# Routing counts in two products, LayerNorm in single-tile pieces, urgent first experts, and the last group's second experts in two halves

## The chip, the core and the metric

The kernel runs on one core of one Trainium2 chip. The metric is device time in microseconds (us), the median of several runs. Engines: TensorE (PE, matmuls; PEld is its weight load), VectorE (DVE), ScalarE (ACT), GpSimd (POOL), and SyncE (SP), which issues most of the DMAs.

## The reference

The input x is 8 sequences of 256 tokens with 128 features, all in float32. Four layers follow one another, each on the LayerNorm of x and added to x:

```python
x = x + attn_a(layernorm(x))      # 8 heads of 64, softmax over the query axis
x = x + ffn(layernorm(x))         # the "first experts"
x = x + attn_b(layernorm(x))      # 16 heads of 8, rotary positions, page mask
x = x + ffn(layernorm(x))         # the "second experts", same weights
```

The feed-forward layer sends each token to one of 8 experts:

```python
logits = x_flat @ w_gate + b_gate
route_p, route_idx = max(softmax(logits)), argmax(softmax(logits))
h = relu(einsum('nd,edm->enm', x_flat, W1) + b1)      # m = 512
y = einsum('enm,emd->end', h, W2) + b2
out = y[route_idx, arange(n)] * route_p
```

## The kernel before

The 2048 tokens are worked in 4 groups g of 512 tokens (2 sequences, NT = 4 tiles of 128). Tokens of different groups never meet, so the layers of different groups can overlap. Two main flows run on PE one after the other. `flow_a` (line 609) runs the first attention of all groups, head by head: scores S_a, their maxima on DVE, exponentials on ACT, the division on POOL (vh_a), and the products pav_a. `flow_b` (line 1082) runs the second attention in entries (g, b), b being the sequence of the group, four steps each: S_b for the row maxima, ptop_b, ST_b for the exponentials, and acc_b. Everything else is a *side job*: a Python generator that emits some instructions at a time and yields the time at which it can go on.

The order of the instructions on each engine is fixed when the program is written out. The class `Plan` (line 68) keeps an estimated clock for each engine, with prices for operations and HOP = 0.2 us for a hand-over between engines. After each piece of a flow, `fill` lets side jobs step until a budget of planned PE time is used (BESIDE_A = 2.0 us per head, BESIDE_B = 1.75 us per half step). `step_side` (line 466) takes, of the jobs that are due, the one with the lowest rank: CLOSE (end of an attention), PREPARE (`prepare_a`, `prepare_b`: LayerNorm, projections and layout for the next group), SETUP, and then EXPERTS in order of creation. `finish_sides` runs what is left after the flows.

An expert job (`ffn_pieces`, line 812; jobs f0 to f3 for the first experts, e0 to e3 for the second) has these steps:
- LayerNorm (st, mv, rstd by a power on POOL, h), transposed (pt) to hT, gate product pg, and the chosen expert as a 0/1 matrix eq.
- Counting (`before`): one product with the matrix `earlier` gives each token its place among those of its tile; three products with `ones` add the counts of earlier tiles; four more sum all counts, for the check against the capacity CAP of 128 rows per expert. These are 8 matmuls, 16 PE instructions in the trace.
- Scatter: four indirect DMAs on POOL (tx<-hf) put tokens into a DRAM buffer, 512 rows for each expert; the first 128 rows of each were filled with zeros once at the start. There are two such buffers, used in turn. Two DMAs on SP bring 128 rows of each expert back (rows).
- Once the job before has finished its products: turning (prt, rT), for each expert the hidden product H (4 weights of W1, 128 rows), relu on DVE or ACT (for experts 2, 3, 6 and 7 ACT, but in f0 and f1 all on DVE), and the product py with W2. A relu on DVE is a maximum with -b1 (h_f, h_e), so its missing bias, b1 times W2, is added to b2 beforehand (`second_biases`, pc, b2c; the rest uses b2x).
- Way back: ys is stored to DRAM by SP (ox), four indirect DMAs on POOL gather it by token (yg), and DVE adds it to x.

A job may do its LayerNorm, counts and scatter when the job before the previous one has finished its products (line 813). f(g) is created when the attention of group g is closed; e(g) when the second attention of group g is divided and projected (`divide`, line 1192). The first preparation for `flow_b` (`first_b`) waits for f0. If any count exceeded CAP, a dense version of everything would run at the end under `tc.If`.

```python
        ripe = [side for side in sides if side.due <= now]
        if not ripe or plan.next_free(pm, "m", 3) > now:
            return False
        min(ripe, key=lambda side: side.rank).step()
```

Of the kernel before, what the change touches and what calls it, by code (L numbers as in the profile page):

```python
# [17 lines left out]
P = 128  # L18
# [6 lines left out]
def kernel(  # L25
# [38 lines left out]
    TG = NT * P  # L64
    CAP = P


    class Plan:
# [3 lines left out]
        HOP = 0.2  # L72
# [60 lines left out]
        def matmul(self, out, lhsT, rhs, passes):  # L133
# [4 lines left out]
            if form != self.form:  # L138
                price += 0.15
# [3 lines left out]
        def elementwise(self, engine, op, outs, ins):  # L143
            n = max(ap.free_size() for ap in outs + ins)
            if engine == "dve":
                price = 0.08 + 0.00108 * n
                if op == "reciprocal":
                    price = 0.1 + 0.0067 * n
                elif op in ("bn_stats", "bn_aggr"):
                    price = 0.2  # L150
            elif engine == "act":
                price = (0.2 + 0.00078 * n) + (0.1 if len(outs) > 1 else 0.0)
            else:
                price = 0.2 + 0.002 * n if op != "tensor_tensor" or n > 8 else 1.0
# [120 lines left out]

    b2x = const.tile([P, E, D], F32, tag="b2x", name="b2x")
    load(b2x, b2.partition_broadcast(P))

# [18 lines left out]
    region = const.tile([P, E], F32, tag="region", name="region")  # L297
    closer = const.tile([P, E], F32, tag="closer", name="closer")
# [4 lines left out]

    to_expert = [hbm.tile([E, TG, D], F32, tag=f"tx{b}", name=f"tx{b}") for b in range(2)]
    of_expert = [hbm.tile([E * CAP, D], F32, tag=f"ox{b}", name=f"ox{b}") for b in range(2)]
# [4 lines left out]
    def setup_experts():  # L310
        DVE.tensor_scalar(region, first, -float(TG), float(TG * E), ALU.mult, ALU.add)
        DVE.tensor_scalar(
            closer, first, float(TG - CAP), -float((TG - CAP) * E), ALU.mult, ALU.add
        )
        for b in range(2):
            load(
                to_expert[b][:, 0:CAP, :].rearrange("e c d -> c e d"),
                zeros.unsqueeze(1).to_broadcast([P, E, D]),
            )

# [8 lines left out]
    b2c = const.tile([P, E, D], F32, tag="b2c", name="b2c")  # L329

    def second_biases():
        for k in range(E // 4):
            pc = misc(f"pc_{k}")
            for i in range(4):
                e = 4 * k + i
                for m in range(NM):
                    c = e * NM + m
                    PE.matmul(
                        pc[:, ts(i, D)], lhsT=b1T[:, c : c + 1].to_broadcast([P, P]),
                        rhs=W2_sb[:, e, m, :], start=(m == 0), stop=(m == NM - 1),  # L340
                    )
# [1034 lines left out]
```

## Time and profile before

| | us |
|---|---|
| median of 3 runs | 554.19 (551.46 to 554.21) |
| profiled execution, device time | 557.06 |
| its span, first to last instruction | 555.3 |
| PE busy | 447.0 (80%) |
| PE weight load busy | 349.0 (63%) |
| DVE busy | 290.4 (52%) |
| ACT busy | 215.6 (39%) |
| POOL busy | 171.5 (31%) |
| mean granted PE clock | 0.879 |

The profile is of one execution. A page of it gives the busy share of each engine in 40 slices of 13.9 us, in tenths. A table of stretches gives the busy time of each engine between chosen times. The chain of waits follows the last instruction back to what released it: each line has a start, a length and the engine and tile that held the chain; "issue" is time for which the profile shows no cause. All compute instructions have the same source line (a helper), so they are told apart by the names of their tiles. Names that are used below: S_a, pav_a first attention; S_b, ST_b, ptop_b, acc_b second attention; before, tx, rows, prt, H, py, ox, yg the expert jobs, with _f and _e for first and second.

### The profile page before, as it was taken

How to read it: one execution, taken by the hardware profiler on the slowest of the kernel's cores; microseconds unless marked ns; L12 is line 12 of the kernel's file. 1: busy time of each engine (PE TensorE's matmuls, PEld its weight loads, DVE VectorE, ACT ScalarE, POOL GpSimd, SP SyncE). 2: the span in 40 equal slices, each digit the busy share in tenths (PEclk: the TensorE clock that was granted, in tenths of full speed). 3: DMA queues.
4: the chain of work that ended last, by engine and by line, in shares of the span. 5: the costliest groups of instructions: out<-in, count | busy, mean ns of one | idle time of the engine just before them, and what ended most of it. 6: DMA issues, size and time to landing. Idle time of an engine off the chain costs nothing.

```text
span 555.3 us, 13517 instructions
## 1 busy us (share of the span) xinstructions
PE 447.0 (80%) x5694; PEld 349.0 (63%) x5694; DVE 290.4 (52%) x742; ACT 215.6 (39%) x591; POOL 171.5 (31%) x227
## 2 busy tenths in 40 slices
PE   3998769678996499998999997999969997392740
PEld 2775546455895388775677865768847875392740
DVE  2576674556752458546675655666427464222110
ACT  1454563545701133555355534266413433230210
POOL 4032330632406454136404420234260012306020
PEclk9996988879995599999899997699978999596785
DMA  7920000010011301101010010010030001202111
GB/s 218 318 77 4 2 1 3 21 41 2 2 33 45 96 1 50 30 1 39 21 41 1 20 30 11 11 48 2 21 95 21 21 20 39 58 19 77 38 49 34
DMA packets 32644, 23.04 MB, mean 41 GB/s; under 512 B 2712, under 2 KB 29888, under 8 KB 32576
## 3 DMA queue, kind: packets, MB, share of 16 engines
q1 hardware_dynamic: 30528, 17.90, 11.0%
q0 software_dynamic: 2048, 4.20, 2.7%
q8 instruction: 47, 0.77, 0.6%
q14 instruction: 21, 0.17, 0.1%
HBM read 13.70 MB, written 8.39 MB: 40 GB/s over the span
## 4 chain that ended last, share of the span: by engine, by line
PE 64%; DVE 14%; issue 7%; ACT 5%; DMA 4%; POOL 4%; another core or an unknown queue 1%; POOLq 0%; SPq 0%; ACTq 0%; DVEq 0%
PE ST_b L201 8%; PE acc_b L201 7%; PE pq_a L201 6%; PE H_e L201 6%; PE py_e L201 5%; PE H_f L201 5%; PE py_f L201 5%; PE S_a L201 3%; PE prot_b L201 3%; PE S_b L201 3%; ACT ex_a L201 2%; DVE nmax_a L201 2%; DVE top L201 2%; PE ptop_b L201 2%; PE pav_a L201 2%
## 5 line engine op out<-in xcount | busy, mean ns | idle before, releaser
L201 ACT ACTIVATE bex_b<-ST_b 128x768 f32<-128x768 f32 x64 | 51.7, 810 | 99.3 <-PE S_b L201 89.1
L201 DVE TENSOR_REDUCE top<-S_b 128x2 f32<-128x256 f32 (+1 forms) x128 | 65.2, 553 | 39.8 <-PE S_b L201 32.1
L201 PE MATMUL ST_b<-qT_b,kT_b 32*128 32x128 f32 (+1 forms) x512 | 71.3, 368 | 11.1 <-ACT bex_b L201 7.2
L201 ACT ACTIVATE ex_a<-S_a,nmax_a 128x256 f32<-128x256 f32 x128 | 58.8, 476 | 38.8 <-DVE nmax_a L201 22.0
L201 PEld LDWEIGHTS ST_b<-qT_b,kT_b 32*128 32x128 f32 x512 | 52.8, 196 | 26.0 <-ACT bex_b L201 12.4
L201 PE MATMUL S_b<-kT_b,qT_b 32*128 32x128 f32 (+1 forms) x512 | 61.8, 366 | 3.6 <-DVE top L201 3.5
L201 POOL TENSOR_TENSOR vh_a<-vs_a,rden_a 128x512 f32<-128x512 f32 x32 | 33.3, 1044 | 93.2 <-DVE rden_a L201 72.5
L201 PEld LDWEIGHTS S_b<-kT_b,qT_b 32*128 32x128 f32 x512 | 48.1, 196 | 7.2 <-issue 6.8
L201 DVE TENSOR_REDUCE nmax_a<-S_a 128x4 f32<-128x1024 f32 x32 | 38.8, 1214 | 7.9 <-PE S_a L201 7.1
L201 PE MATMUL S_a<-qT_a,kT_a 64*128 64x256 f32 x256 | 37.5, 411 | 4.3 <-ACT ex_a L201 3.6
L201 PE MATMUL H_e<-rT_e,W_sb 128*128 128x128 f32 x256 | 35.6, 290 | 0.0
L201 PE MATMUL H_f<-rT_f,W_sb 128*128 128x128 f32 x256 | 34.0, 278 | 0.0
L201 PEld LDWEIGHTS H_e<-rT_e,W_sb 128*128 128x128 f32 x256 | 33.1, 205 | 1.3 <-issue 0.9
L201 PE MATMUL py_f<-W_sb,h_f 128*128 128x128 f32 x256 | 33.7, 277 | 0.0
L201 PE MATMUL py_e<-W_sb,h_e 128*128 128x128 f32 x256 | 33.3, 276 | 0.0
L201 PEld LDWEIGHTS H_f<-rT_f,W_sb 128*128 128x128 f32 x256 | 31.0, 192 | 2.5 <-issue 2.0
L201 PE MATMUL acc_b<-bex_b,sum_w 128*32 128x128 f32 (+1 forms) x512 | 30.8, 346 | 1.3 <-issue 1.2
L201 PEld LDWEIGHTS py_f<-W_sb,h_f 128*128 128x128 f32 x256 | 30.9, 192 | 1.1 <-issue 0.7
L201 POOL DMA_INDIRECT yg_e<-ox,posi_e x16 | 15.5, 970 | 50.7 <-DMA ox<-ys_e 46.5
L201 PEld LDWEIGHTS py_e<-W_sb,h_e 128*128 128x128 f32 x256 | 30.7, 192 | 0.6 <-issue 0.6
L201 PE MATMUL acc_b<-bex_b,vz 128*32 128x128 f32 (+1 forms) x512 | 30.1, 354 | 0.9 <-issue 0.8
L201 PEld LDWEIGHTS S_a<-qT_a,kT_a 64*128 64x128 f32 x256 | 22.4, 190 | 11.6 <-ACT ex_a L201 5.9
(193 smaller groups left out, 798.2 us busy)
## 6 DMA issues: line engine op xcount, KB each, us to landing
W_sb<-in_L_ffn_W_dram SPq DMA_DIRECT2D x16, 256.0 KB, 6.2
rows_f<-tx SPq DMA_DIRECT2D x8, 256.0 KB, 3.5
ox<-ys_f SPq DMA_DIRECT2D x8, 256.0 KB, 2.4
rows_e<-tx SPq DMA_DIRECT2D x8, 256.0 KB, 2.9
ox<-ys_e SPq DMA_DIRECT2D x8, 256.0 KB, 2.3
x_in<-in_L_attn_a_x_dram SPq DMA_DIRECT2D x4, 256.0 KB, 3.4
tx<-zeros SPq DMA_DIRECT2D x2, 512.0 KB, 8.0
out_dram<-x_e SPq DMA_DIRECT2D x4, 256.0 KB, 2.3
```

The source lines that it names most:

```text
L201: return tc.keep_in_program_order(getattr(self.engine, op)(*args, **kw))
```

## The change

- Counting takes two products over a matrix of 5 columns of blocks: `earlier` with eqs (eq and a zero block), and `ones` with sums, a running sum over tiles that DVE builds by a copy and three additions. The last block of the result is the total count. POOL zeroes one block of eqs and one of sums.
- LayerNorm yields after each tile's statistics and each tile's normalization.
- A rank URGENT is put ahead of all others. f0 gets it, and so does `first_b`. URGENT and CLOSE jobs may step when the filling budget is used up. f(g) is created when group g begins its first attention and waits for its input (x_of); `first_b` is created when group 3 begins its first attention. For it, `prepare_b` adds the extra rows with one DVE instruction instead of ACT and POOL.
- The last group's second experts become two jobs of 256 tokens (2 tiles), e30 and e31, each with 64 rows per expert; `divide` gives the first its input after the group's first entry. e(g) is created when group g begins its second attention.
- Each job has DRAM buffers of its own, with its own zeros loaded at its first step. Experts are worked in pairs. rT has one buffer instead of two. The relu of experts 0, 1, 4 and 5 is on DVE and that of the others on ACT in all jobs, and bias2 takes the place of b2x and b2c, made from four loads and 16 instead of 32 matmuls. Tiles u1 to u3 of the preparation share the three vh buffers of the first attention.
- HOP and some prices of the planner have new values.

```diff
-        HOP = 0.2
+        HOP = 0.3
...
-                price += 0.15
+                price += 0.2
...
+    ROWS = {4: 128, 2: 64}
...
+    def on_vector(e):
+        return e // 2 % 2 == 0
...
     def second_biases():
-        for k in range(E // 4):
-            pc = misc(f"pc_{k}")
-            for i in range(4):
-                e = 4 * k + i
-                for m in range(NM):
-                    c = e * NM + m
-                    PE.matmul(
-                        pc[:, ts(i, D)], lhsT=b1T[:, c : c + 1].to_broadcast([P, P]),
-                        rhs=W2_sb[:, e, m, :], start=(m == 0), stop=(m == NM - 1),
-                    )
...
-            DVE.tensor_tensor(
-                b2c[:, half, :], b2x[:, half, :], pc.rearrange("p (e d) -> p e d", e=4), ALU.add
+        pairs = b2.rearrange("(k i) d -> k i d", i=2)
+        for parts, place, i in PARTS:
+            load(
+                bias2[parts, :, place, :],
+                pairs[:, i, :].partition_broadcast(parts.stop - parts.start),
             )
-            yield
+        yield hop()
+        pc = misc("pc")
+        chosen = [e for e in range(E) if on_vector(e)]
+        for k, e in enumerate(chosen):
+            for m in range(NM):
+                c = e * NM + m
+                PE.matmul(
+                    pc[:, ts(k, D)], lhsT=b1T[:, c : c + 1].to_broadcast([P, P]),
+                    rhs=W2_sb[:, e, m, :], start=(m == 0), stop=(m == NM - 1),
+                )
+        for parts, place, i in PARTS:
+            mine = bias2[parts, 0 : E // 2 : 2, place, :]
...
+            DVE.tensor_tensor(mine, mine, added, ALU.add)
+        yield
...
     sides = []
...
-        if now >= until or max(plan.at["dve"], plan.at["act"]) > now + LATE:
+        if max(plan.at["dve"], plan.at["act"]) > now + LATE or plan.next_free(pm, "m", 3) > now:
             return False
         ripe = [side for side in sides if side.due <= now]
-        if not ripe or plan.next_free(pm, "m", 3) > now:
+        if not ripe:
             return False
-        min(ripe, key=lambda side: side.rank).step()
+        side = min(ripe, key=lambda side: side.rank)
+        if now >= until and side.rank > CLOSE:
+            return False
+        side.step()
...
         for i in range(NT):
             st = sm.tile([P, 6], F32, tag="st", name=f"st_{name}_{i}")
             DVE.bn_stats(st, xt[:, i, :])
             DVE.bn_aggr(mv[:, i, :], st)
+            yield
...
+        PT = 2 * CAP // P
+        to_expert = hbm.tile([E, TL, D], F32, tag=f"tx_{n}", name=f"tx_{n}")
+        of_expert = hbm.tile([E * CAP, D], F32, tag=f"ox_{n}", name=f"ox_{n}")
+        for c in range(0, CAP, P):
+            some = min(P, CAP - c)
+            load(
+                to_expert[:, c : c + some, :].rearrange("e c d -> c e d"),
+                zeros[0:some].unsqueeze(1).to_broadcast([some, E, D]),
+            )
         while computed[0] < turn - 1:
             yield soon()
-        xt, buf = xs[g], turn % 2
-        n = f"{n}{g}"
+        while any(name not in x_of for name, _ in tokens):
+            yield soon()
...
-        lg, d, eq, sc, ex, rk = (small(s) for s in ("lg", "d", "eq", "sc", "gex", "rk"))
+            return t.unsqueeze(1).to_broadcast([P, NL, E])
+        lg, d, sc, ex, rk = (small(s) for s in ("lg", "d", "sc", "gex", "rk"))
+        eqs, sums = (
+            sm.tile([P, NT + 1, E], F32, tag=f"r{s}", name=f"{s}_{n}", bufs=2)[:, 0 : NL + 1, :]
+            for s in ("eq", "sums")
+        )
+        POOL.memset(eqs[:, NL, :], 0.0)
+        POOL.memset(sums[:, 0, :], 0.0)
+        eq = eqs[:, 0:NL, :]
...
+        yield
+        DVE.tensor_copy(sums[:, 1, :], eq[:, 0, :])
+        for i in range(1, NL):
+            DVE.tensor_tensor(sums[:, i + 1, :], sums[:, i, :], eq[:, i, :], ALU.add)
         yield hop()
-        before = misc(f"before_{n}")
-        PE.matmul(
-            before[:, : NT * E], lhsT=earlier, rhs=eq.rearrange("p n e -> p (n e)"),
-            start=True, stop=False,
-        )
-        for i in range(NT - 1):
+        before = misc(f"before_{n}")[:, 0 : (NL + 1) * E]
+        for lhsT, of, start in ((earlier, eqs, True), (ones, sums, False)):
             PE.matmul(
-                before[:, (i + 1) * E : NT * E],
-                lhsT=ones,
-                rhs=eq[:, i : i + 1, :].to_broadcast([P, NT - 1 - i, E]),
-                start=False,
-                stop=(i == NT - 2),
+                before, lhsT=lhsT, rhs=of.rearrange("p n e -> p (n e)"), start=start,
+                stop=not start,
             )
-        counts = before[:, NT * E : (NT + 1) * E]
-        for i in range(NT):
-            PE.matmul(
-                counts, lhsT=ones, rhs=eq[:, i, :], start=(i == 0), stop=(i == NT - 1)
-            )
+        counts = before[:, NL * E : (NL + 1) * E]
         DVE.tensor_tensor(
-            rk, before[:, : NT * E].rearrange("p (n e) -> p n e", e=E), over_tiles(region),
-            ALU.add,
+            rk, before[:, : NL * E].rearrange("p (n e) -> p n e", e=E),
+            over_tiles(region[NL]), ALU.add,
         )
         DVE.tensor_tensor(rk, rk, eq, ALU.mult)
         DVE.tensor_reduce(ps_, rk, AX.X, ALU.add)
...
-        rows = ln.tile([P, E, D], F32, tag="rows", name=f"rows_{n}", bufs=3)
-        for k in range(2):
-            half = slice(k * E // 2, (k + 1) * E // 2)
...
+        pairs = to_expert.rearrange("(k i) c d -> i c k d", i=2)
+        tiles_of = rows[:, 0 : PT * E // 2, :].rearrange("p (k t) d -> p k t d", t=PT)
...
             load(
-                rows[:, half, :],
-                to_expert[buf][half, 0:CAP, :].rearrange("e c d -> c e d"),
+                tiles_of[p0 : p0 + some, :, t, :],
+                pairs[r0 // CAP, r0 % CAP : r0 % CAP + some, :, :],
             )
...
-        rT = ln.tile([P, E * CAP], F32, tag="rT", name=f"rT_{n}", bufs=2)
-        ys = ln.tile([P, E, D], F32, tag="rows", name=f"ys_{n}", bufs=3)
+        rT = ln.tile([P, TILES * P], F32, tag="rT", name=f"rT_{n}", bufs=1)
...
-            h1 = big.tile([P, NM, CAP], F32, tag="h1r", name=f"h1_{n}_{e}", bufs=4)
-            H = misc(f"H_{n}_{e}")
-            for m in range(NM):
...
+            h1 = big.tile([P, NM, P], F32, tag="h1r", name=f"h1_{n}_{e}", bufs=4)
+            some = min(NM, 512 // CAP)
+            for m0 in range(0, NM, some):
+                H = misc(f"H_{n}_{e}_{m0}")
+                for m in range(some):
+                    PE.matmul(
+                        H[:, ts(m, CAP)], lhsT=W1_sb[:, e, ts(m0 + m, P)],
+                        rhs=rT[:, ts(e, CAP)], start=True, stop=True,
+                    )
+                c = e * NM + m0
...
+                for t in range(t0, t1):
+                    r0 = t * P
+                    if r0 // CAP == (r0 + 64) // CAP:
+                        parts = [(h1s[r0 // CAP][:, :, r0 % CAP : r0 % CAP + P], slice(0, P))]
+                    else:
+                        parts = [
+                            (h1s[r // CAP][:, :, r % CAP : r % CAP + 64], slice(p0, p0 + 64))
+                            for r, p0 in ((r0, 0), (r0 + 64, 64))
+                        ]
+                    for m in range(NM):
+                        for part, to in parts:
+                            e = 2 * k + (r0 + to.start) // CAP
+                            PE.matmul(
+                                py[to, ts(t - t0, D)], lhsT=part[:, m, :],
+                                rhs=W2_sb[:, e, m, :], start=(m == 0), stop=(m == NM - 1),
+                            )
...
+        pending = None
+        for k in range(E // 2):
+            h1s = []
+            for e in (2 * k, 2 * k + 1):
+                h1s.append(hidden(e))
+                yield
+            if turns and turns[0] < (k + 2) * PT:
+                turned(turns.pop(0))
+                yield
+            if pending:
+                yield max(plan.over(h1.name) for h1 in pending[1]) + plan.HOP
+                yield from project(*pending)
+            pending = k, h1s
+        yield max(plan.over(h1.name) for h1 in pending[1]) + plan.HOP
+        yield from project(*pending)
         computed[0] += 1
...
+            yield hop() if i == NL - 1 else None
+        at = 0
+        for (name, tiles), xt in zip(tokens, xts):
+            xn = new_x(f"x_{n}_{at}")[:, 0:tiles, :]
...
-                t.append(mid.tile([P, 2, T], F32, tag=f"u{y + 1}", name=f"rt_{n}_{w}_{y}", bufs=1))
+                t.append(mid.tile([P, 2, T], F32, tag="vh", name=f"rt_{n}_{w}_{y}", bufs=3))
...
-            rt = mid.tile([P, 2, T], F32, tag="u3", name=f"rt_{n}_{w}", bufs=1)
+            rt = mid.tile([P, 2, T], F32, tag="vh", name=f"rt_{n}_{w}", bufs=3)
...
-                ACT.mul(xT[:, r, :, :], rt, section[r])
-                yield hop()
-                POOL.tensor_tensor(
-                    xT[:, r, :, :], xT[:, r, :, :],
-                    extra[:, w, r : r + 1, :].to_broadcast([P, 2, T]), ALU.add,
-                )
+                rows = extra[:, w, r : r + 1, :].to_broadcast([P, 2, T])
+                if at_once:
+                    DVE.scalar_tensor_tensor(
+                        xT[:, r, :, :], rt, section[r], rows, ALU.mult, ALU.add
+                    )
+                else:
+                    ACT.mul(xT[:, r, :, :], rt, section[r])
+                    yield hop()
+                    POOL.tensor_tensor(xT[:, r, :, :], xT[:, r, :, :], rows, ALU.add)
...
-            if b == 1:
-                yT = yTs[g].rearrange("p b t -> p (b t)")
-                py = misc(f"py_b{g}")
-                for i in range(NT):
...
+            whole = g != groups[-1] or len(groups) == 1
+            if whole and b == 0:
+                return
+            tiles = range(NT) if whole else range(2 * b, 2 * b + 2)
+            yT = yTs[g].rearrange("p b t -> p (b t)")
+            py = misc(f"py_b{g}_{b}")
+            for k, i in enumerate(tiles):
+                PE.matmul(
+                    py[:, ts(k, P)], lhsT=yT[:, ts(i, P)], rhs=wo_sb, start=True, stop=True
                 )
...
+            some = slice(tiles[0], tiles[-1] + 1)
+            xn = new_x(f"x_b{g}_{b}")[:, 0 : len(tiles), :]
...
+            x_of["e", g if whole else (g, b)] = xn
...
     def first_experts(g):
-        share = set(range(E)) if g < 2 else {0, 1, 4, 5}
-        ready[g] = Side(ffn(g, "f", share, g < 2), EXPERTS + begun_ffn[0])
...
+        def ended(name, rows):
+            x_of["b", name[1]] = rows
+        Side(ffn(f"f{g}", [(("f", g), NT)], ended, g < 2), URGENT if g == 0 else EXPERTS + g)
...
+    def second_experts(name, *tokens):
+        def ended(name, rows):
...
+        Side(ffn(name, tokens, ended, False), EXPERTS + begun_ffn[0])
+    def begun_a(g):
         if g == 0:
             setup_experts()
             ready["bias"] = Side(second_biases(), SETUP)
...
+        first_experts(g)
         if g == NG - 1:
-            ready["first"] = Side(first_b(), PREPARE)
+            ready["first"] = Side(first_b(), URGENT)
+    def begun_b(g):
+        if g < NG - 1:
+            second_experts(f"e{g}", (("e", g), NT))
+            return
+        for b in range(2):
+            second_experts(f"e{g}{b}", (("e", (g, b)), 2))
...
-        return (yield from prepare_b(0))
+        return (yield from prepare_b(0, True))
```

## The prediction

> **What bounds the kernel now.** I read the busy share first, then the same engines by stretch, then the chain that ended last. The page's slices:
>
> ```profile
> PE   3998769678996499998999997999969997392740
> ...
> PEclk9996988879995599999899997699978999596785
> ```
>
> TensorE (PE) is at 9 or near it nearly everywhere, except for three holes: the first slice, slices 13 and 14 (about 165 to 192 us), and the last six (from 472 us). In the holes the granted clock drops to 0.5 too, so what little runs there runs slower. The stretches put numbers on it (columns: length, then busy time of PE, weight load, DVE, ACT, POOL; the last three are clock, DMA share, GB/s):
>
> ```profile
> 13.00:163.00 150.00, 129.34 (x2177) 94.66 (x2174) 93.56 (x215) 74.74 (x283) 44.03 (x51) 0.91 0.16 48
> 163.00:192.00 29.00, 14.69 (x75) 12.62 (x73) 10.41 (x54) 4.57 (x12) 15.25 (x26) 0.59 0.20 58
> 192.00:212.00 20.00, 20.00 (x142) 17.97 (x145) 11.32 (x21) 7.59 (x20) 11.40 (x10) 0.91 0.13 36
> 212.00:467.00 255.00, 236.01 (x2852) 179.64 (x2848) 150.04 (x374) 111.79 (x232) 76.05 (x89) 0.94 0.10 27
> 467.00:500.00 33.00, 21.86 (x170) 20.89 (x166) 10.61 (x32) 8.68 (x25) 5.69 (x10) 0.79 0.11 32
> 500.00:545.00 45.00, 21.30 (x161) 20.40 (x160) 10.17 (x34) 5.96 (x19) 12.51 (x18) 0.72 0.19 53
> 545.00:555.30 10.30, 0.00 (x0) 0.00 (x0) 0.14 (x1) 0.00 (x0) 0.00 (x0) 0.50 0.12 33
> ```
>
> Both attentions (13 to 163 and 212 to 467) are bound by PE with the side work fed in: 86% and 93% busy. Between them stand 49 us, and behind them 88 us, in which a chain of small steps sets the pace. The chain of waits names them:
>
> ```profile
> 168.24 3.36 PE before_f L201 x16
> ...
> 178.51 5.42 issue
> ...
> 188.91 1.06 POOL rstd_b L201
> ...
> 211.81 0.94 PE S_b L201 x16
> ...
> 467.74 3.77 issue
> 471.52 1.01 POOL tx L201
> ...
> 516.60 1.94 PE prt_e L201 x8
> ...
> 534.20 2.28 DMA ox<-ys_e
> ```
>
> The first product of the second attention (S_b) stands at 211.81, because its input is the output of group 0's first experts, and these were served last: their tokens are back in rows at 114, but their products H_f run from 139.5, and POOL normalizes the result (rstd_b) at 188.9, behind eight scatters of groups 1 and 2. The tail is: dispatch of group 2's second experts until 480.7 (13.0), their products until 498.7 (17.9), dispatch of group 3 until 516.6 (17.9), products until 533.7 (17.1), way back until 545.2 (11.5), end (10.1).
>
> **Part 1: urgent first experts.** f0 becomes a side job of the highest rank, created when group 0 begins, and steps past the allotted filling time; b0's preparation (first_b) gets the same rank when group 3 begins, near 118. x_a of group 0 is there near 46 (pt_a at 44.07). Dispatch of f0 takes about 18 (group 3's, above), products 17 if nothing stands between, way back about 10, so x_f0 comes near 95 to 110, before 118. b0's preparation, with extra rows added by one fused DVE instruction instead of ACT and POOL (0.72 + 1.16 each, eight of them), then lies in group 3's attention. So S_b can follow the first attention directly. What f0 moves past: its four scatters (1.28 each) and rstd (1.04) stand on POOL among the heads' vh_a products of group 1 instead of group 2 (105 to 110 now), where POOL is as idle (44 of 150 us); its loads and stores on SP pass only loads that are done by 40. The price there stays what it was: 0.
> Where does that end? Now near 163. Added on PE: b0's transposes, values and rotations, 4 instructions 0.45 (full clock), 8 in 0.9, 8 in 3.5, together about 5. Removed: half of second_biases, one of two blocks of 32 instructions of 3.77 us, on the chain at 23 and 29; and 1.5 of f0's counts (part 2). Taken: plus 3 for new waits, of which two are not in the trace. The rotations' tiles now share the three vh buffers with the heads (bounds 0 to 8: six tiles, each waiting at most for one pav of 1.1 us and the POOL product of 1.04; behind the waiting DVE instruction stand the heads' maxima). And DVE's bias sums now wait for four loads issued near 21 instead of one at 19.4 (0 to 5: the W loads take 6.2 us to land and the zeros 8.0). S_b at 163 + 5 - 3.8 - 1.5 + 3 = 166, instead of 211.8: **-46**.
> That isn't all gain: in those 49 us PE also did f1 and f2's dispatch. At full clock: turning 1.0, H 7.2 (64 instructions, 0.89 per 8), py 7.2, transposes, gates and counts of f1 and f2 3.8. **+19** must be paid again in the second attention, which is dense: 1 for 1.
>
> **Part 2: counts by two products.** Each of eight dispatches issues 16 PE instructions now, 4 after. On the chain 16 cost 1.95 at full clock and 3.36 to 3.5 at half. So 1.5 to 2.6 each are saved. DVE pays a copy and three sums, 0.22 a step on the chain (0.66 to 0.9), beside PE's other work in the attentions and open in the tail. f0 to f2 are counted already; f3, e0, e1, e2 and e3 give 5 x 1.6 = **-8** (bounds -4 to -12). Two POOL memsets (0.09 each, from mark) come into the wait of the product: see the third rival. LayerNorm by single tiles adds no instruction; it only lets other work between.
>
> **Part 3: zeros and buffers.** The zero loads go from 2 to 9, 8.0 us each to landing (half that for a half group), on SP and the DMA engines, which are at 0 to 3 tenths after 42 us. They are issued at a job's first step, before it waits for its input, and the first scatter comes 10 us or more after LayerNorm starts; I take 0. If SP stood behind a waiting store (its waits on ys_f reach 46.1) a scatter would be late by up to 8. Relu of experts 2, 3, 6, 7 of f0 and f1 moves to ACT (4 x 0.37 instead of 0.69 each, 6 us more on ACT per group); ACT has 75 of 150 us there: 0. One rT buffer instead of two: products of two groups never overlap: 0.
>
> **Part 4: the last group in halves.** Per half as many H and py instructions as for a whole group, with 64 rows. H: weights are the same 128x128, and the weight load's row (8 in 0.97) is as long as the matmul's (8 in 1.06), so the 3.6 a half would cost by columns is likelier 6: between 0 and +7.2 for both, taken +5. py: 64 columns wide, two side by side (0 to +7.2, taken +2). Changes of form: 8 py after attention's acc_b take 1.09 in the chain and 0.89 after H, so 0.20 a change, 16 changes: +3.
> The Trainium skill (TensorEngine Tiling (Array Packing), Key Properties) says the same of the last: changing the mode drains TensorE; and its Instruction Overhead gives each matmul about 60 cycles of overhead, so that 64 columns gain little. That speaks against halves; by it, as an estimate, +7 for H would stand in the place of +5. No row here has 64 columns at 128 rows, so nothing in this trace tests it.
> The tail then, from attention's end, if the backlog is the same as now: e2's dispatch 11 (13 less 2 for counts), products 17.9, first half's dispatch 13.5 (17.9 - 2.3 counts + 0.5 sums - 2 scatters of 1.28), its products 11.5 (17 x half, +3), second half's dispatch 11 (2 gathers of 1.26 fewer ahead of it), products 11.5, way back 8.9, end 10.1: 95 with nothing overlapped, 82 with the first half's dispatch behind e2's products. The first half's input is there one entry of attention (some 30 us) before the end, but its rank is below e2's, and e2 is nearly always ready. Middle: 88, as now: **0**.
>
> **Sum.** 555.3 - 46 + 19 - 8 + 0 = 520.3; stalls I haven't placed (the planner's prices and its HOP are all new, so each engine's order changes; the PE holes of 20.7 and 19.0 us inside the attentions could shrink or grow) I leave at +2: span 522. The profiled execution took 557.06 for a span of 555.3; the median of the runs is 554.19, 1.1 below the span. So **521 us**, -6%. Fallback to the dense path is excluded: counted from the reference's inputs, the fullest expert gets 50 tokens of a half (limit 64) and 92 of a group (limit 128).
>
> **Rivals.**
> *The halves overlap.* If f0's early end also drags e0 to e2 forward, so that e2 is done and the first half dispatched when attention ends, the tail is the second half alone: division and LayerNorm 9, dispatch 11, products 11.5, back 8.9, end 10.1, about 51 to 70 for 88: 485 to 508, taken 502. For it: attention takes in side work for only 88 of 255 us. Against: the 19 us of part 1 come first.
> *Moved, not saved.* f1's work pushes e1 past the attention's end; the tail holds e1's products (18) as well and each dispatch is open: 521 + 18 = 539.
> *POOL comes between.* The product of the counts now needs two POOL memsets. POOL is in order, and a job's gathers stand and wait for the store ("POOL yg_e" waits 46.5 us in two stretches for ox). If a memset falls behind four gathers, PE, in order too, waits 2.3 + 4 x 1.26 = 7.3. At all eight later dispatches that is 58: 579, slower. It decides from the fifth on (5 x 7.3 = 36 against 33 gained). Against it: the memsets are emitted with the gate product, some 2 us before the counts, mostly ahead of the gathers.
> *The change doesn't do what it says:* f0 urgent, but b0 still late (S_b near 200): 545; this and the second rival share a place.
>
> **How the numbers follow.** Forecast (510 to 533) 0.50; halves overlap (below 510) 0.20; moved or not urgent in effect (533 to 551) 0.18; POOL between (above 557) 0.08; in the last 0.04 they cancel. Within 0.5% (551.4 to 557.0), about what a measurement of this kernel can tell from none, 0.04. Faster 0.88, slower 0.08. The range, 8 in 10: down to 498, up to 545, from part 4's and the second rival's bounds.
>
> **What would show it.** S_b's first product near 166 and no hole at slices 13 and 14; `before` at 4 instructions a job and about 0.5 us at full clock; the PE holes left only in the tail; py of the halves near 6 us a half; tail 82 to 95. Wrong if PE waits for POOL at `before`, if S_b starts after 190, or if the tail is outside 65 to 105.

## The result and the profile after

The kernel after takes 581.0 us (median of 4 runs, 576.14 to 582.13), before 553.38 in the same series: ratio 1.0487, 95% interval 1.0418 to 1.0557. It is slower by 4.9%; the prediction was 521. The profiled execution took 576.14 for a span of 574.3.

The slices of the page after:

```profile
PE   3879688999777899789799997889959986995690
...
PEclk9999889899886599879799996799988999698555
```

The hole at slices 13 and 14 is narrower, as meant. What is new stands to its right: 7s and 8s among the 9s of slices 16 to 29 (215 to 416 us), where before has one 8 and one 7, and clocks of 6 to 8 beside them. The same stretches as before (length, then busy time of PE, weight load, DVE, ACT, POOL; clock, DMA share, GB/s):

```profile
167.00:183.40 16.40, 8.32 (x142) 5.36 (x140) 14.30 (x33) 5.00 (x24) 7.25 (x10) 0.68 0.00 1
183.40:485.40 302.00, 267.75 (x2970) 201.14 (x2970) 167.45 (x442) 120.01 (x258) 91.22 (x131) 0.89 0.10 30
485.40:510.00 24.60, 20.58 (x148) 19.99 (x148) 9.73 (x33) 6.33 (x21) 2.46 (x5) 0.79 0.16 50
510.00:537.00 27.00, 14.85 (x144) 12.91 (x142) 8.68 (x41) 5.81 (x22) 9.26 (x15) 0.83 0.21 64
537.00:574.30 37.30, 21.85 (x129) 20.30 (x129) 4.06 (x13) 4.17 (x17) 1.93 (x2) 0.55 0.06 16
```

The second attention starts at 183.4 instead of 211.8 (-28.4), but takes 302.0 instead of 255.3 (+46.7); the tail takes 88.9 instead of 88.2. That is +19.0, the whole difference of the spans. In the second attention PE is busy 31.5 us more, idle 34.3 instead of 19.0, and the clock falls from 0.94 to 0.89.

The list of what PE waits for in this stretch (total, times, longest) has three rows that before does not have there at all:

```profile
PE pt_f L203 <- ACT hf_f L203: 4.4, 2, 3.7
PE pt_b L203 <- ACT h_b L203: 4.0, 2, 3.0
PE pt_e L203 <- ACT hf_e L203: 2.4, 3, 1.3
```

PE waits 10.8 us in front of LayerNorm transposes whose rows are still being made. The timeline shows the longest of them:

```profile
240.85 0.79 PE L203 MATMUL prt_f<-ident,rows_f 128*128 128x128 f32 x4
...
244.65 0.13 DVE L203 SCALAR_TENSOR_TENSOR shift_f<-mv_f,rstd_f 128x4 f32<-128x4 f32 x1
244.82 1.65 ACT L203 ACTIVATE hf_f<-x_a,shift_f,rstd_f 128x128 f32<-128x128 f32 x4 [2.56 <-DVE shift_f L203]
...
245.37 1.63 PE L203 MATMUL pt_f<-ident,hf_f 128*128 128x128 f32 x4 [3.73 <-ACT hf_f L203]
```

The transposes stand in PE's written order when not one row of hf_f exists: the first is begun at 244.82. None of the attention's products that are written behind them starts before them, and PE does nothing for 3.73 us; then the four transposes go at ACT's pace (1.63 for four; 0.66 where the rows are ready, pt_b at 236.38 in the mended kernel below).

Why do they stand there? The code of after says it:

```python
        def step(self):
            plan.end = 0.0
            try:
                self.due = max(next(self.gen) or 0.0, plan.at["pe"])
...
    def hop():

        return plan.end + plan.HOP
...
            yield
        yield hop()
        pt = misc(f"pt_{name}")
```

`hop()` is meant to be the planned end of the last instruction of this step plus HOP. With LayerNorm in pieces, the last piece ends its step with a plain `yield`. The next step zeroes `plan.end`, issues nothing, and yields 0 + 0.3: due at once. The planned wait between the normalisation and the transposes is gone. I call it the lost hop.

### The profile page after: what moved, and what is told of

It is laid out like the page before. It is cut to its first block, busy times and chain, and to the rows that moved or that the text cites. A ratio compares the mean times of both kernels' runs of the same rounds, so it can differ in the third digit from the quotient of the medians.

```text
span 574.3 us, 13668 instructions
## 1 busy us (share of the span) xinstructions
PE 468.1 (82%) x5698; PEld 355.4 (62%) x5698; DVE 302.6 (53%) x805; ACT 221.4 (39%) x633; POOL 164.2 (29%) x240
## 5 line engine op out<-in xcount | busy, mean ns | idle before, releaser
L203 DVE TENSOR_REDUCE top<-S_b 128x2 f32<-128x256 f32 (+1 forms) x128 | 65.1, 553 | 47.7 <-PE S_b L203 37.2
L203 PE MATMUL S_b<-kT_b,qT_b 32*128 32x128 f32 (+1 forms) x512 | 69.1, 402 | 6.1 <-DVE top L203 5.5
L203 PE MATMUL H_e<-rT_e,W_sb 128*128 128x128 f32 (+1 forms) x320 | 48.7, 317 | 2.8 <-ACT rT_e L203 2.8
L203 PEld LDWEIGHTS H_e<-rT_e,W_sb 128*128 128x128 f32 x320 | 46.0, 230 | 5.8 <-ACT rT_e L203 4.0
L203 PE MATMUL S_a<-qT_a,kT_a 64*128 64x256 f32 x256 | 43.4, 460 | 7.6 <-ACT ex_a L203 7.1
L203 POOL DMA_INDIRECT yg_e<-ox_e,posi_e x16 | 15.6, 976 | 76.6 <-DMA ox_e<-ys_e 73.0
L203 PEld LDWEIGHTS S_a<-qT_a,kT_a 64*128 64x128 f32 x256 | 25.6, 214 | 17.1 <-ACT ex_a L203 9.0
L203 PE MATMUL pav_a<-ex_a,vh_a 128*32 128x64 f32 x1024 | 24.7, 244 | 12.3 <-POOL vh_a L203 5.5
L203 PE MATMUL py_e<-W_sb,h_e 128*128 128x128 f32 (+1 forms) x320 | 34.6, 304 | 0.0
L203 ACT ACTIVATE h_e<-H_e,b1T 128x128 f32<-128x128 f32 (+1 forms) x80 | 20.5, 354 | 36.0 <-PE H_e L203 36.0
L203 PEld LDWEIGHTS pav_a<-ex_a,vh_a 128*32 128x32 f32 x1024 | 18.8, 123 | 24.8 <-POOL vh_a L203 12.7
L203 PEld LDWEIGHTS py_e<-W_sb,h_e 128*128 128x128 f32 (+1 forms) x320 | 31.9, 187 | 0.7
```

The source lines that it names most:

```text
L203: return tc.keep_in_program_order(getattr(self.engine, op)(*args, **kw))
```

## The experiments

Before itself took 541 to 557 us on the chips used, so kernels are compared by their ratio to before in the same series (95% interval in brackets), and stretches from the profiled executions. "S_b" is the start of the second attention, "B" its length. The ratio of one and the same kernel moved by a point between two chips (0.9696 and 0.98, the counts alone, below), so differences of about a point between two series can't be told from none.

### First series: one part of after undone

*The old planner numbers* (HOP and prices of before):

```diff
-        HOP = 0.3
+        HOP = 0.2
...
-                price += 0.2
+                price += 0.15
...
```

> The kernel after, with the planner's numbers of before alone put back (HOP 0.2, a change of form 0.15, and its old ScalarE, VectorE and GpSimd prices); all instructions are those of after, only their order differs. Theory 1 (the new prices spread the side work wrongly: of the +46.7 us in the second attention 28 are idle gaps and half clock that the written order makes): 555 to 565 us, the stretch from the first S_b to the last acc_b 275 to 285 instead of 302. Theory 2 (the work itself, its place and the buffers it shares are what costs): 576 to 586, the stretch 297 to 307. Theory 3 (the halves of the last group): 576 to 586 as well.

Measured: 1.0512 (1.0488 to 1.0536). The first theory falls: the prices are not what costs.

*No urgency:*

```diff
-        if now >= until and side.rank > CLOSE:
+        if now >= until:
...
-URGENT if g == 0 else EXPERTS + g)
+EXPERTS + g)
...
-            ready["first"] = Side(first_b(), URGENT)
+            ready["first"] = Side(first_b(), PREPARE)
```

> The kernel after, without the urgent rank: first experts of group 0 take rank EXPERTS + 0, the first preparation of the second attention PREPARE, and no side steps past its budget. Theory 1 (prices): 578 to 590, since the first S_b falls back from 183 towards 200 while the second attention keeps its gaps. Theory 2 (the urgent steps push the heads of the first attention aside and leave work for the second): first S_b at 195 to 212, the second attention 302 shorter by 19 to 35, total 565 to 581. Theory 3 (halves): no change beyond 5 us either way.

Measured: 1.0416 (1.0362 to 1.0469). S_b 207.2 instead of 183.4, B 276.4 instead of 302.0: what the urgent rank wins ahead of S_b (23.8) is paid back behind it (25.6).

*The last group whole:*

```diff
-            whole = g != groups[-1] or len(groups) == 1
+            whole = True
...
-        for b in range(2):
-            second_experts(f"e{g}{b}", (("e", (g, b)), 2))
+        second_experts(f"e{g}", (("e", g), NT))
```

> The kernel after, with the last group's second experts and its close in one piece of four tiles as in before; everything else as after. Theory 1 and 2: the tail from the last acc_b to the end stays at 85 to 100 us (88.9 with halves, 88.2 before), the second attention shortens by at most 8 (the first half's work leaves it: its rows, products of 14 us at most), total 572 to 590. Theory 3 (128 hidden products of 64 columns at 350 ns, bound by their weights and at half clock, and two chains of dispatch in place of one are the loss): tail 88 with 25 us of work less elsewhere, total 552 to 562.

Measured: 1.0285 (1.0256 to 1.0315), tail 87.9 against 88.9. The halves fill 13 us of the tail's idle time (44.5 whole, 31.7 halved) with 14 us more of PE work. Faster than after, as the first two theories allowed; the next series shows whether that lasts.

*Experts one at a time* in whole groups, three pending:

```diff
...
+            for e in range(E):
+                queue.append((e, hidden(e)))
+                yield
+                if len(queue) == 3:
+                    yield from project_next()
...
```

> The kernel after, with the experts of all whole groups taken one at a time with three pending, and both transposes ahead of them, as in before (the second products of a pair of experts came in one step of 16 products in after); the halves stay in pairs. Theory 1 (prices): within 8 us of 581. Theory 2 in its sharper form (a step of 16 products, about 4.5 us in one go, starves the attentions between their heads): 560 to 572, the gaps and the half-clock time of the second attention (34.3 and 64.6) halfway back to 19.2 and 30.7. Theory 3: within 5 us of 581.

Measured: 1.0701 (1.0666 to 1.0736). All three theories missed: slower, B 302.7, tail 107.0 with a clock of 0.60. None of the four brings after back to before.

### Second series: the lost hop

*The hop mended*, everything else as after:

```diff
-            yield
+            if i < NT - 1:
+                yield
         yield hop()
```

> The kernel after, with one line changed: the LayerNorm on ScalarE or VectorE still comes in pieces of one tile, but the last piece does not end its step, so that the hop to the transposes is counted from that piece. Theory L (in after the step behind the last piece issues nothing, its hop is counted from a zeroed end, and the transposes are put into PE's order before their rows are there: 10.8 us of waits of pt_f, pt_b and pt_e in the second attention, none in before): these waits fall below 3 us, the stretch from S_b to the last acc_b from 302 to 285 to 293, total 564 to 573. Rival O (the wait only moves to the next product that PE needs, since the rows come no sooner): the waits fall, the stretch stays within 5 of 302, total 576 to 584.

Measured: 1.0017 (0.9975 to 1.006), 556.6 us: more than expected, 4.7 points by two lines. The stretches of the mended kernel, the one row of transposes left in PE's waits in its second attention, and the largest row there:

```profile
20.70:184.00 163.30, 126.73 (x2135) 91.08 (x2135) 106.09 (x281) 83.33 (x315) 57.63 (x76) 0.92 0.19 54
184.00:463.80 279.80, 256.83 (x2950) 195.61 (x2950) 168.38 (x434) 117.38 (x253) 86.76 (x120) 0.91 0.10 30
463.80:554.70 90.90, 65.83 (x419) 60.44 (x419) 21.49 (x75) 16.25 (x58) 13.55 (x22) 0.63 0.13 37
```

```profile
PE pg_e L203 <- ACT hT_e L203: 7.3, 2, 5.2
...
PE pt_f L203 <- ACT hf_f L203: 1.8, 1, 1.8
```

S_b stays at 184.0; B falls by 22.2. Of these, 11.3 are idle time (34.3 to 23.0) and 8.5 are speed: PE spends 47.7 us at half clock instead of 64.6. The theory that the wait only moves (rival O) is right in a small part: 7.3 us of waits stand now in front of the gate product pg_e, 0 in after. In the longest, 5.2, the copy hT_e stands on ACT behind gex_e, which waits for d_e on POOL, behind four scatters (455.58 to 460.45).

*LayerNorm undivided* (both piece-wise `yield` lines taken out):

```diff
             DVE.bn_aggr(mv[:, i, :], st)
-            yield
...
-            yield
         yield hop()
```

> The kernel after with the LayerNorm undivided: no step ends between its statistics or between its four normalisations, as in before. Theory L: the same gain as with the last hop mended, within 4 us of that kernel (564 to 573). A theory of its own (pieces as such help: shorter steps let the attention's reductions and exponentials in between): slower than the mended kernel by 4 to 12 us. Rival O: 576 to 584.

Measured: 1.0074 (1.0046 to 1.0103), 4 us above the mended kernel. Undoing the pieces also restores the hop; pieces as such are worth little.

*Mended and whole* (both edits above): 

> The kernel after, with the last hop of the LayerNorm mended and the last group's second experts whole. If the two losses are separate (11 us for the halves by the ratios 1.0487 and 1.0285, and 8 to 17 for the lost hop): 553 to 562. If the order alone decides and both were chance: 568 to 578.

Measured: 1.0 (0.9957 to 1.0044), as the mended kernel with halves. The halves' 2 points of the first series do not add: on the mended kernel they are worth nothing either way.

*The pieces alone, on before:*

```diff
             DVE.bn_aggr(mv[:, i, :], st)
+            yield
...
                     bias=shift[:, i : i + 1], scale=rstd[:, i : i + 1],
                 )
+            yield
         yield hop()
```

> The kernel before, with the LayerNorm in pieces as in after and nothing else. Theory L: waits of the transposes behind their rows appear in the second attention (0 us in before), 6 to 12 us of them, total 562 to 572 where before has 554 to 557. Rival O: within 4 us of before.

Measured: 1.0222 (1.018 to 1.0264), with 9.8 us of transposes' waits in B where before has none:

```profile
PE pt_f L201 <- ACT hf_f L201: 4.8, 1, 4.8
...
PE pt_e L201 <- ACT hf_e L201: 2.8, 3, 1.7
...
PE pt_b L201 <- ACT h_b L201: 2.2, 2, 1.9
```

So these waits come with the lost hop from both sides; with the pieces and their hop on before (third series) no such row stands in the second attention. The price of the hop is shown on after alone: in the 12 us here the pieces themselves have a share, since with their hop they cost 9 us on the counts base.

### Third series: counts, zeros and urgency

*Mended, without urgency* (the edits of both kernels above):

> The kernel after with the last hop of the LayerNorm mended (556.6 us) and without the urgent rank. Theory M (urgency moves work and saves none: the 27.8 us that the first S_b comes earlier are paid again in the second attention, 24.5, and in the tail, 2.7): first S_b at 198 to 210, the second attention 255 to 268, total 551 to 561. Rival W (urgent first experts are worth what the first S_b gains, and something else in after eats it): total 570 to 584.

Measured: 1.0099 (1.0054 to 1.0144); S_b 205.2, B 269.4, tail 83.6. Mended with urgency it was 1.0017. Theory M holds within a point, with B 1.4 above its range.

*The counts alone, on before:*

```diff
...
+        POOL.memset(eqs[:, NT, :], 0.0)
+        POOL.memset(sums[:, 0, :], 0.0)
...
+        for lhsT, of, start in ((earlier, eqs, True), (ones, sums, False)):
+            PE.matmul(
+                before, lhsT=lhsT, rhs=of.rearrange("p n e -> p (n e)"), start=start,
+                stop=not start,
+            )
...
```

> The kernel before with the counts by two products over a running sum and nothing else. By the prediction's term (30 of 32 products of 0.2 to 0.6 us leave PE, 22.5 us of records to 8): 543 to 553, against 555 for before. Rival O (PE waits for the longer chain on VectorE and for the zeros that GpSimd writes): 553 to 563.

Measured: 536.5 us, 0.9696 (0.9617 to 0.9774). More than the term: B 242.1 instead of 255.3, half clock in it 13.7 us instead of 30.7.

*Mended, the zeros written by VectorE:*

```diff
-        POOL.memset(eqs[:, NL, :], 0.0)
-        POOL.memset(sums[:, 0, :], 0.0)
+        DVE.memset(eqs[:, NL, :], 0.0)
+        DVE.memset(sums[:, 0, :], 0.0)
```

> The kernel after with the last hop mended, and the two zeroed columns of every dispatch written by VectorE instead of GpSimd. If the zeros behind the gathers on GpSimd hold up the counts (the third rival of the prediction): the waits of before_e and before_f behind eq and sums go, 546 to 553. If they do not matter: within 3 us of 556.6.

Measured: 1.0116 (1.0074 to 1.0158): no gain. The one wait of `before` behind POOL in the mended kernel (3.5 us) is gone, the time is not: the zeros behind the gathers do not decide.

*Counts and mended pieces on before* (the edits shown above, together):

> The kernel before with two parts of the change: the counts by two products, and the LayerNorm in pieces with the hop counted from its last piece. If the two parts add (counts -2 to -12, pieces with their hop -5 to +2): 541 to 555, and faster than both kernels. If any change of the written order costs as much as it brings: 554 to 564.

Measured: 0.9855 (0.9775 to 0.9935). Faster than both kernels, but slower than the counts alone (545.5 against 536.5 us in the same series): the pieces bring nothing even with their hop.

### Fourth series: single parts on the counts base

With the hop mended after is still 2 to 3 points above before with the counts. Each of the next kernels adds one part to that base. Urgency:

```diff
...
-        ready[g] = Side(ffn(g, "f", share, g < 2), EXPERTS + begun_ffn[0])
+        ready[g] = Side(job, URGENT if g == 0 else EXPERTS + begun_ffn[0])
...
```

> The kernel before with the two-product counts (536.5 us), and with the urgent part alone: first experts of group 0 and the first preparation of the second attention in the urgent rank, the rule that urgent steps may pass their budget, and the first preparation's columns made at once on VectorE. Theory M (moved, not saved): first S_b 20 to 30 us earlier than 206.5, the second attention longer by as much, total 532 to 541. Theory P (the prediction's term: 46 won, 19 paid): 505 to 515. Theory U (urgency is the 20 us that after still lacks): 546 to 560.

Measured: 1.0024 (0.9997 to 1.0051). S_b 187.3, B 268.9.

The planner's numbers of after:

```diff
-        HOP = 0.2
+        HOP = 0.3
...
```

> The kernel before with the two-product counts, and the planner's numbers of after (HOP 0.3 and the new prices). If these write the worse order: 545 to 560. If they do not matter: 533 to 541.

Measured: 0.9841 (0.9793 to 0.9889): no loss that can be told.

Experts in pairs:

```diff
...
+        def project_pair(k, h1s):
+            yield max(plan.over(h1.name) for h1 in h1s) + plan.HOP
+            for e, h1 in zip((2 * k, 2 * k + 1), h1s):
+                project(e, h1)
+            yield
...
```

> The kernel before with the two-product counts, and the experts taken in pairs as in after: 16 second products in one step, the second transposes behind the first pair. If the long steps hold up the attentions: 542 to 556, with more waits and more half clock in the second attention (17.1 and 13.7 us). If the pairs help, as the run with single experts in after (595 against 581) says: 526 to 536.

Measured: 1.0109 (1.0063 to 1.0156). B 256.5.

Shared buffers:

```diff
-tag=f"u{y + 1}", name=f"rt_{n}_{w}_{y}", bufs=1
+tag="vh", name=f"rt_{n}_{w}_{y}", bufs=3
...
-tag="rT", name=f"rT_{n}", bufs=2
+tag="rT", name=f"rT_{n}", bufs=1
```

> The kernel before with the two-product counts, and the shared buffers of after: the rotated products of the second attention's preparation in the three buffers of vh, one buffer in place of two for the turned rows of the experts. If the sharing is what after lacks: 545 to 558, with waits of pav behind vh or of rt behind pav in the first attention's last group. If not: 533 to 541.

Measured: 0.9769 (0.9722 to 0.9815), the lowest median of all, 529.2 us, and 7% below after (1.0487) by ratio. Against the counts base (0.9696 and, on another chip, 0.98) sharing costs nothing.

### Fifth series: the pairs taken from the mended kernel

Both edits (hop mended, experts one at a time) on after, and the counts base on the same chip:

> The kernel after with the last hop mended, and the experts of whole groups taken one at a time with three pending. If the pairs' long steps are what the mended kernel still lacks: its ratio to before falls from 1.002 to 0.965 to 0.985. If the worth of pairs hangs on the order around them (they cost 19 us on the counts base and brought 14 on after): ratio 0.99 to 1.03.

> The kernel before with the two-product counts, once more, on the chip that runs the kernel beside it: ratio 0.965 to 0.980 to before; with it the gap of the mended kernel to the counts base is read on one chip.

Measured: 0.9855 (0.977 to 0.994) and 0.98 (0.9746 to 0.9854). The gap is closed to half a point. The stretches of the first, from S_b on:

```profile
178.70:423.80 245.10, 232.81 (x2889) 179.34 (x2889) 158.99 (x409) 114.55 (x241) 76.79 (x102) 0.99 0.09 29
423.80:529.60 105.80, 64.90 (x481) 60.11 (x477) 26.70 (x103) 20.32 (x70) 23.06 (x39) 0.70 0.15 46
```

and of the counts base:

```profile
207.20:444.40 237.20, 222.30 (x2800) 169.75 (x2801) 154.14 (x391) 114.02 (x242) 79.05 (x99) 0.97 0.10 29
444.40:529.00 84.60, 39.51 (x301) 37.43 (x301) 22.39 (x75) 14.66 (x44) 18.29 (x30) 0.73 0.16 45
```

With both mends B holds f1 and f2's work in 245.1 us at a clock of 0.99, 57 us less than after. The early S_b is then real: the attention ends 20.6 us before that of the counts base. The tail takes 21.2 more, because the second experts of the later groups are no further: when the attention ends, the last of e1's products are still running, and all of e2, e30 and e31 stands behind it: e2's hidden products start 22 us after the end, where those of the counts base start 15 after it, and the last half's at 489.9.

## Why the prediction was wrong, step by step

Three steps failed. The one that made the kernel slower is the LayerNorm in pieces, which the prediction had at nothing: "LayerNorm by single tiles adds no instruction; it only lets other work between", and beside it "stalls I haven't placed ... I leave at +2". No instruction was added, but a wait in the written order was taken away. Measured: +25 us in after (1.0487 against 1.0017). Among kernels with single experts the lost hop is worth more, 8 points (1.0701 against 0.9855). It could have been read from the diff: a bare `yield` now stands ahead of `yield hop()`, and what `hop` adds to is zeroed at each step.

With the hop mended the kernel is only as fast as before, so two more steps are needed for the gain that did not come. The largest is the term for urgency, -46 + 19 = -27: what it wins ahead of S_b is paid again in full behind it (-23.8 and +25.6 in after), and by ratio it is worth between -0.8 and +2.2 points. The other was not priced at all: experts in pairs, 16 second products in one step. They cost 3 points on the counts base (1.0109 against 0.98, and against 0.9769 on the same chip) and 1.6 on the mended kernel (1.0017 against 0.9855, on two chips). In the kernel with the lost hop they brought 2 points; why the sign turns there is not settled.

Point by point:
- *S_b at 166* (-46): 183.4 (-28.4). "x_a of group 0 is there near 46 (pt_a at 44.07)" misread a row: that pt_a is the LayerNorm transpose of group 1. The closing of group 0's attention, also named pt_a but fed by yT_a, is at 71, and the first tile of x_f0 is added at 136.5 instead of 95 to 110 (before 183.3). S_b follows the last pav_a directly, as predicted, but the first attention itself ends at 183.4 instead of 158.6. I had added 5 for b0's preparation and 3 for waits. PE shows 8.3 and 10.5 there, 6.0 more of f0's and f1's work, and 7.7 more in S_a and pav_a themselves; 7.7 less in other rows, 3.7 of it in second_biases, stand against these.
- *+19 paid again:* the first experts' work on PE in B rose from 37.5 to 55.9, +18.4. The size was right, "1 for 1" was not: on the counts base B grew by 31.7 (237.2 to 268.9), with 15.8 of such work, 11.1 more idle time and 12.8 more at half clock.
- *-46 + 19 = -27 for urgency:* 0.7 points slower on after, 0.8 faster on the mended kernel (neither can be told from none), 2.2 slower on the counts base. "Moved, not saved" is the rival that came true, but not in its place: the work lengthened the second attention and did not push e1 into the tail. The range of the first rival, the halves that overlap, has a slip: 521 less 88 and with 51 to 70 gives 484 to 503, not 485 to 508.
- *Counts -8* (bounds to -12): -11 to -17 by the two ratios of the counts base. `before` on PE fell from 22.5 to 7.2 us in the eight dispatches; the term counted five of them. In B, 17 us less at half clock are worth another 8.5, which the term did not have; how far the two overlap is not separated.
- *Zeros, buffers 0:* right for the buffers (0.9769 against 0.98). No wait of PE in after is put down to a zero load. The relu split was not tried by itself.
- *Halves 0 in the tail:* right in sum, 88.9 against 88.2, partly by luck. The second half's products took 21.5 us at half clock instead of 11.5 and its dispatch 15.0 instead of 11; the first half's dispatch was hidden, e2's took 6.8 instead of 11, and way back and end 15.3 instead of 19. Over both halves H took 11.1 a half instead of 6, py 5.7, as predicted:

```profile
L203 PE MATMUL H_e<-rT_e,W_sb 128*128 128x128 f32 x192 | 26.5, 295 | 1.4 <-ACT rT_e L203 1.4
...
L203 PE MATMUL H_e<-rT_e,W_sb 128*128 128x64 f32 x128 | 22.2, 350 | 1.4 <-ACT rT_e L203 1.4
...
L203 PE MATMUL py_e<-W_sb,h_e 128*64 128x128 f32 x128 | 11.5, 346 | 0.0
```

  Much of that is the half clock. In the mended kernel with single experts the same 32 instructions of 64 columns take 3.79 us at full clock and 7.09 at half. From start to start they are 0.112 apart at full clock, and so are those of 128 columns; at half clock both are 0.213 apart. The Trainium skill (TensorEngine Tiling (Array Packing), Instruction Overhead) gives each matmul about 60 cycles of overhead, which speaks for a small gain from so few columns; here they gain nothing.
- *POOL comes between (579):* the number was nearly hit, but by luck: in after no wait of PE at `before` is put down to POOL, and with the zeros on VectorE nothing is won. Such waits do occur elsewhere (before_f behind POOL's sums_f: 2.8 us in the first run of the counts base, 6.1 in the second), and both runs are faster than before.

What stays open: why single parts of a written order change their worth, and even their sign, with what stands around them. Mended pieces cost 1.6 points on the counts base and bring 0.6 on after; no experiment tells which neighbour decides. The same pair of yields stands, in both kernels, ahead of POOL's sum of the rotations in `prepare_b`; it was not tried either.

## What to carry to other kernels

Where the order of an engine's instructions is written by hand, a change that adds no instruction can still take away a wait: check for each `yield` what the next due time is counted from, and look in the trace for products that stand ahead of their inputs. Price a moved piece of work at its new place with that place's gaps and clock, not one for one. Try each part of a bundle alone: the counts by themselves bring 2 to 3%, and the rest of this change costs more than that.

## What the runs showed of the hardware

The granted clock has two values in the records, 1 and 0.5, and changes in steps of 3.41 us. The time at half clock goes by and large with the span: 90 us (span 529.6, mended with single experts), 104 (529.0, counts base), 134 (555.3, before), 141 (554.7, mended), 139 (572.5, no urgency), 152 (574.3, after), 181 (590.9, single experts with the lost hop). I cut the trace of after into its windows of 3.41 us: no window at full clock with more than 1.61 us without PE records was followed by another; the 19 falls came after 1.25 to 3.02 us of it, in one gap or several together. The clock came back after a window with at most 0.07 (in before once after 0.85), but not after every such window. In before, the mended kernel and the one with single experts, the largest idle time in a window that kept the clock was 1.5 to 1.7, and 4 of 32 falls came after less than 1.0. So in these four traces 2 us of waits within one window were always enough, and they are paid for twice: as idle time, and as half speed behind it.

The Trainium skill (TensorE: Matmul & The Clock Gate, "Why this matters for your kernels") asks for no PE-idle gaps over about 3 us. The window of 3.41 us agrees with its Part 1. The threshold does not: 13 of the 19 falls in after came with no gap over 3 us, and the measurement decides.
